# Two 256-column parts of neighbouring head groups computed as one unit of attention scores

## The chip, the core and the metric

The kernel runs on one core of a Trainium2 chip. The metric is the device time of one execution in microseconds (us). The kernel before was timed in three runs: 3645.09, 3648.94 and 3651.80 us, so its median is 3648.94 us. One further execution was profiled; the profile calls the engines PE (TensorE, the matrix engine), DVE (VectorE), ACT (ScalarE), POOL (GpSimd) and SP (SyncE, which issues the DMAs here).

## What is computed

The reference is one transformer block whose norms and residuals are modulated by a condition. Cut to what matters (D = 512, 16 heads of 32 columns, x of shape 8 x 1024 x 512, all in fp32):

```python
def _attention(x, Wqkv, Wproj, bproj):
    ...
    scores = jnp.einsum('bhqd,bhkd->bhqk', q, k) * scale
    causal = jnp.tril(jnp.ones((t, t), bool))
    scores = jnp.where(causal, scores, -jnp.inf)
    attn = jax.nn.softmax(scores, axis=-1)
    ...
    return out @ Wproj + bproj
mod = jax.nn.silu(condition) @ Wada + bada
sh_a, sc_a, gt_a, sh_m, sc_m, gt_m = jnp.split(mod, 6, axis=1)
xm = _layernorm(x, g1, be1) * (1.0 + sc_a[:, None, :]) + sh_a[:, None, :]
x = x + gt_a[:, None, :] * _attention(xm, Wqkv, Wproj, bproj)
xm = _layernorm(x, g2, be2) * (1.0 + sc_m[:, None, :]) + sh_m[:, None, :]
h = jax.nn.gelu(xm @ W1 + b1, approximate=False)
x = x + gt_m[:, None, :] * (h @ W2 + b2)
```

## The kernel before

**Tiling.** The work is cut into 16 blocks of 512 tokens (8 sequences, two halves each). The 16 heads form 4 groups of 4 heads. A head has 32 columns, so the four heads of a group lie on the 128 partitions side by side, and every matmul of the kernel is issued as four small ones that use a quarter of the array each.

**Two kinds of work on PE.** The linear layers (q, k, v, the projection and the two MLP layers, most of them in a scheme with seven products for eight) all go through the helper at L201: tiles of 128 rows and 32 columns of the array, "128*32" in the profile. The scores go through tiles of 32 rows and 128 columns, "32*128" in the profile. Transposes (L641) use the whole array. A run of instructions that all use one of these three shapes is called a stretch below.

**Attention of one group of heads of one block.** It is computed twice. First come the *scores*, which serve only to find the maximum of each row: for each query tile of 128 rows, `scores_at_once` (L1372) writes scores of the four heads into one PSUM tile with the tag `st` (four banks; there is only one such tile), DVE adds the causal mask at the diagonal (L1384) and takes the maxima into the tile `mx` (L1392). Then `split_maxima` (L1406 to L1414) cuts the maxima of a group into three bf16 parts, on DVE or on POOL, whichever the planner believes to be done sooner; PE turns them into rows (L1430) and ACT copies these to SBUF (L1436). Second come the *weights*, transposed: `weights_T` computes the same products with keys as rows (L1456) and subtracts the maxima by a bf16 matmul (L1467), again in the one tile `st`; ACT takes the exponential into a tile `pT` (L1479), POOL clears the part above the diagonal (L1484) and adds the tiles up (L1611), and PE multiplies by v (L1507). `finish` divides by the sums (L1525 to L1557).

**Units.** What is written into `st` at once is a unit. The causal triangle of 512 queries by 512 keys of a group makes three units of scores: query tile 3 with 512 keys; tiles 2 and 0 together with 384 and 128 keys; and tile 1 with 256 keys alone, the half-filled unit. `TRIANGLE` lists them. A block that is the second half of its sequence has four full units more for each group. With 64 groups in all (16 blocks by 4) the profile shows 64 units of 256 columns. The code addresses a part of a unit as (query tile, half of the keys, first column, width).

**What sets the order.** The program is straight-line code. A planner runs when the program is built: it keeps an estimated clock for each engine (`now`), estimated times at which data are written and free (`written`, `left`), and places pieces of linear work (`work`, `step_aside`) between the attention's instructions so that PE has something to do while DVE, ACT or POOL work on `st`. How many units of scores follow a unit of weights is set by `attend`, by the number of units. Engines execute their instructions in the order of the program. If linear work runs out, `scores_by_heads` (L1343) spreads a unit over the three other PSUM banks instead of `st`. For the planner, NEVER marks data that nobody has promised yet; `project_out` of the last block sets it for ("att", last block, tile), and `finish` of the last group replaces it by a time.

Of the kernel before, what the change touches and what calls it, by code (L numbers as in the profile page):

```python
# [9 lines left out]
F32 = mybir.dt.float32  # L10
BF16 = mybir.dt.bfloat16
AF = mybir.ActivationFunctionType
ALU = mybir.AluOpType
AX = mybir.AxisListType
# [8 lines left out]
def kernel(  # L23
# [33 lines left out]
    nc = tc.nc  # L57
    B, T, D = x.shape
    HD = W1.shape[1]
    P = 128  # L60
    hd = D // H
    scale = float(hd) ** -0.5
    TB = 512
    NTT = TB // P
# [3 lines left out]
    HPG = P // hd  # L68
# [13 lines left out]
    small = ctx.enter_context(tc.tile_pool(name="small", bufs=2))  # L82
# [8 lines left out]
    NB = len(blocks)  # L91
# [3 lines left out]
    written, left = {}, {}  # L95
    shape = [None]
    pool_spans = []
    NEVER = float("inf")
# [66 lines left out]
    banks = [ps_l.tile([P, TB], F32, tag=f"l{i}", name=f"bank_{i}") for i in range(3)]  # L165
# [72 lines left out]
    for w in range(1, NB):  # L238
        n = w - 1
# [10 lines left out]
        else:  # L250
# [5 lines left out]
            at = [("at", w + 2)] if w + 2 < NB else []  # L256
# [8 lines left out]
    n = NB - 1  # L265
# [621 lines left out]
    def project_out(n):  # L887
        at = take(NC)
        yield [("attended", n)], []
        attT = qTs[n]  # L890
        tiles = [residual[n][:, t, :] for t in range(NTT)]
        for t, xt in enumerate(tiles):
            xt_job = lambda t=t, xt=xt: add_to(xt, gate_rows["gba"], [("row", "gba")], [("xr", n, t)])
            pool_jobs.append((xt_job, [("xr", n, t)]))
        last = n == NB - 1
        if last:
            for t in range(NTT):
                written["att", n, t] = NEVER
        begun = []

        def begin(t):

            bank = yield from accumulate(
                [(attT[:, c, ts(t, P)], piece(at[c])) for c in range(NC - 1)], [("att", n)], False
            )
            begun.append(bank)

        for t, xt in enumerate(tiles):
            if last:
                while len(begun) <= max(t, 1):  # L910
                    yield from begin(len(begun))
                bank = begun[t]
                yield [("att", n, t)], []
                matmul(
                    banks[bank], attT[:, NC - 1, ts(t, P)], piece(at[NC - 1]), False, True,
                    [("att", n, t)], bank,
                )
            else:
                bank = yield from accumulate(
                    [(attT[:, c, ts(t, P)], piece(at[c])) for c in range(NC)], [("att", n)]  # L920
                )
            y = tmp.tile([P, D], F32, tag="y", name=f"y_{n}_{t}", bufs=2)
            ky = y_key("proj", True)
            combine_out(y, bank, banks[bank], gate_rows["ga"], [("row", "ga")], [ky], ALU.mult)
            if last:
                run_pool_jobs(True)
                nc.vector.tensor_tensor(xt, xt, y, ALU.add)  # L927
                note("DVE", 700, [ky, ("xr", n, t)], [("xr", n, t)], port=True)
                following = normalize_tile(xt, f"m{n}", t, ("xr", n, t))
                if t > 0:  # L930
                    pending()
                pending = following
            else:
                add_to(xt, y, [ky], [("xr", n, t)])
        if last:
            pending()
        release(*at)
        run_pool_jobs(True)
        if not last:
            normalize(tiles, f"m{n}", [("xr", n, t) for t in range(NTT)])  # L940
# [336 lines left out]

    def score_units(n, g):

        h = blocks[n][1]  # L1280
        whole = [[(qt, kh, 0, TB)] for kh in range(h) for qt in range(NTT)]
        for tri in TRIANGLE:
            parts, at = [], 0
            for i in tri:
                w = TB - i * P
                parts.append((NTT - 1 - i, h, at, w))
                at += w
            whole.append(parts)
        return [(n, g, parts) for parts in whole]

# [22 lines left out]
    def keys_of(n, kh):  # L1313
        return kTs[n - blocks[n][1] + kh]

    def scores(n, g, parts):

        h = blocks[n][1]
        if (n, g) not in maxima:
            maxima[n, g] = small.tile([P, 2, NTT, HPG], F32, tag="mx", name=f"mx_{n}_{g}")  # L1320
        mx = maxima[n, g]
        reads = [("qT", n), ("kT", n - h + parts[0][1])]
        if (
            linear_wait() > 3000
            and not any(live)
            and wait_of((reads, ["st"])) > wait_of((reads, [BANK])) + 1000
        ):
            scores_by_heads(n, g, parts, mx, reads)
        else:
            scores_at_once(n, g, parts, mx, reads)  # L1330
        if units[unit_at[0] + 1 :] == [] or units[unit_at[0] + 1][:2] != (n, g):
            split_maxima(n, g, h)

    def scores_by_heads(n, g, parts, mx, reads):

        h = blocks[n][1]
        for some in (range(HPG - 1), range(HPG - 1, HPG)):
            step_aside(reads, [BANK])
            of = {j: lin_bank() for j in some}
            for qt, kh, c0, w in parts:  # L1340
                for j, bank in of.items():
                    r = slice(j * hd, (j + 1) * hd)
                    nc.tensor.matmul(  # L1343
                        banks[bank][:, c0 : c0 + w],
                        qTs[n][r, g, ts(qt, P)],
                        keys_of(n, kh)[r, g, :w],
                        start=True,
                        stop=True,
                        skip_group_check=True,
                    )  # L1350
                note_pe(2 * COLUMN * w, "rows", reads, [("l", bank) for bank in of.values()])
            for j, bank in of.items():
                if parts[0][1] == h:
                    first, span = parts[0][3] - P, len(parts) * P
                    diagonal = banks[bank][:, first : first + span]
                    nc.vector.tensor_tensor(diagonal, diagonal, mask[:, :span], ALU.add)
                    note("DVE", 120 + 1.04 * span, [("l", bank)])
                for qt, kh, c0, w in parts:
                    nc.vector.tensor_reduce(
                        mx[:, kh, qt, j : j + 1], banks[bank][:, c0 : c0 + w], axis=AX.X, op=ALU.max  # L1360
                    )
                    note("DVE", 170 + w, [("l", bank)], [("mx", n, g)])
                live[bank] = False

    def scores_at_once(n, g, parts, mx, reads):
        h = blocks[n][1]
        step_aside(reads, ["st"])
        sc = ps_st.tile([P, HPG, TB], F32, tag="st", name=f"sc_{n}_{g}_{parts[0][0]}_{parts[0][1]}")
        for qt, kh, c0, w in parts:
            for j in range(HPG):  # L1370
                r = slice(j * hd, (j + 1) * hd)
                nc.tensor.matmul(  # L1372
                    sc[:, j, c0 : c0 + w],
                    qTs[n][r, g, ts(qt, P)],
                    keys_of(n, kh)[r, g, :w],
                    start=True,
                    stop=True,
                    skip_group_check=True,
                )
            note_pe(2 * COLUMN * w, "rows", reads, ["st"])  # L1380
        if parts[0][1] == h:
            first, span = parts[0][3] - P, len(parts) * P
            diagonal = sc[:, :, first : first + span]
            nc.vector.tensor_tensor(  # L1384
                diagonal,
                diagonal,
                mask[:, :span].unsqueeze(1).to_broadcast([P, HPG, span]),
                ALU.add,
            )
            note("DVE", 165 + 4.16 * span, ["st"])  # L1390
        for qt, kh, c0, w in parts:
            nc.vector.tensor_reduce(  # L1392
                mx[:, kh, qt, :], sc[:, :, c0 : c0 + w], axis=AX.X, op=ALU.max
            )
            note("DVE", 170 + 4.14 * w, ["st"], [("mx", n, g)])

    def split_maxima(n, g, h):

# [251 lines left out]
        return 600 + 900 * used / TB  # L1650

    def score_need(n, g, parts):
        ns = 300 + sum(100 + 2100 * w / TB for _, _, _, w in parts)
        return ns + (150 + 550 * len(parts) if parts[0][1] == blocks[n][1] else 0)


# [2 lines left out]
    for n in range(NB):  # L1659
        written["attended", n] = NEVER  # L1660
        written["v done", n] = NEVER
        written["m used", n] = NEVER
        if n > 1:
            written["free for v", n] = NEVER
        if n > 2:
            written["free for k", n] = NEVER
    normalize(x_pre.pop(0), "a0", [("x", "a0")] * NTT)
    run_jobs(True)
    open_main([-1], 1.0)
# [65 lines left out]
```

## Time and profile before

| what | value |
|---|---|
| three timed runs, median | 3648.94 us (3645.09 to 3651.80) |
| the profiled execution: its time, its span | 3647.89 us, 3646.2 us |
| PE idle over the span (span less busy time) | 74.6 us |
| DVE, ACT, POOL busy | 2179.1, 1329.2, 2014.6 us |
| instructions on PE (matmuls), DVE, ACT, POOL | 54821, 2501, 1413, 2039 |
| masks added in `st`: 128x512, 128x1024 elements | 128 of 698 ns, 63 of 1230 ns |
| maxima of 256 columns of four heads (128x1024) | 64 of 1225 ns |
| splitting the maxima of a group, four instructions | DVE 42 times, POOL 22 times |
| mean granted clock of PE | 0.995 |

A span is the time from the first to the last instruction of the profiled execution. A group of instructions in the profile is a line of the kernel, an engine, an operation and a form of operands, with how many there were, their busy time in us and the mean of one in ns, and then the idle time of the engine just before them with what ended it. In the trace, an fp32 matmul of the program appears as two, so the four matmuls of one part are "x8". The profile models the end of a matmul; the distance between the starts of two groups is what PE really spent. In a timeline a row has its start in us, its length in us, engine, line, operation, operands and count.

### The profile page before, as it was taken

The numbers are of one execution on the slowest core, as the hardware profiler recorded it, in microseconds if no ns is written. First come the engines' busy times: TensorE is split into PE (matmuls) and PEld (weight loads), VectorE is DVE, ScalarE is ACT, GpSimd is POOL, SyncE is SP. The second block draws the span as 40 slices with busy tenths as digits, with TensorE's granted clock in tenths as the row PEclk, the third lists the DMA queues.
The fourth block names the chain that finished last, engine by engine and source line by source line (L and its number), as shares of the span: only waits on it lengthen the run. The fifth ranks groups of instructions, "written<-read, shape, count | busy, mean of one in ns | idle before, by whom it ended". The sixth has DMA issues, their size and how long they took to land. (4 is left out here: it accounts for less than half of the span.)

```text
span 3646.2 us, 121167 instructions
## 1 busy us (share of the span) xinstructions
PE 3571.6 (98%) x54821; PEld 1770.1 (49%) x54821; DVE 2179.1 (60%) x2501; ACT 1329.2 (36%) x1413; POOL 2014.6 (55%) x2039
## 2 busy tenths in 40 slices
PE   8999999999999999999999999999999999999999
PEld 4434445445554455544545444454544545445445
DVE  6766675564746557465564656746667465664663
ACT  2335234252333523335242352424524244241431
POOL 3656645656455664566636665456654566544560
PEclk9999999999999999999999999999999999999999
DMA  6623333333333343433434334343333433334334
GB/s 220 225 92 104 104 103 109 123 106 119 114 115 112 106 126 111 134 94 104 126 106 143 91 100 123 106 137 103 97 122 110 140 100 103 117 97 143 92 107 138
DMA packets 307894, 430.35 MB, mean 118 GB/s; under 512 B 25900, under 2 KB 176236, under 8 KB 307380
## 3 DMA queue, kind: packets, MB, share of 16 engines
q1 hardware_dynamic: 307264, 422.56, 37.9%
q8 instruction: 432, 7.08, 0.8%
q14 instruction: 82, 0.67, 0.1%
q10 hardware_dynamic: 116, 0.03, 0.0%
HBM read 394.12 MB, written 28.38 MB: 116 GB/s over the span
## 5 line engine op out<-in xcount | busy, mean ns | idle before, releaser
L1611 POOL TENSOR_TENSOR pT<-pT,pT 128x512 f32<-128x512 f32 (+3 forms) x1266 | 1189.2, 973 | 524.9 <-ACT pT L1479 377.1
L1479 ACT ACTIVATE pT<-st 128x2048 f32<-128x2048 f32 (+1 forms) x320 | 546.5, 1708 | 951.3 <-PE st L1467 909.0
L201 PE MATMUL bank<-w,hT 128*32 128x256 f32 x14336 | 808.6, 380 | 2.8 <-DVE hT L1006 2.1
L1392 DVE TENSOR_REDUCE mx<-sc 128x4 f32<-128x1024 f32 (+3 forms) x381 | 664.4, 1757 | 192.4 <-PE sc L1372 185.8
L201 PEld LDWEIGHTS bank<-w,hT 128*32 128x32 f32 x14336 | 452.1, 110 | 354.0 <-issue 58.0
L201 PE MATMUL bank<-xm_m,w 128*32 128x256 f32 x8192 | 506.6, 380 | 0.6 <-ACT rec L1531 0.5
L1484 POOL TENSOR_SCALAR_AFFINE_SELECT pT<-pT 128x512 f32<-128x512 f32 x256 | 175.3, 696 | 576.9 <-ACT pT L1479 576.9
L201 PE MATMUL bank<-t_m,w 128*32 128x256 f32 x6144 | 383.2, 380 | 0.9 <-ACT hT L188 0.9
L201 PEld LDWEIGHTS bank<-xm_m,w 128*32 128x32 f32 x8192 | 253.3, 110 | 252.0 <-issue 98.0
L1456 PE MATMUL st<-qT,kT 32*128 32x512 f32 (+3 forms) x3072 | 339.6, 526 | 21.0 <-DVE mx L1392 20.0
L1372 PE MATMUL sc<-kT,qT 32*128 32x256 f32 (+3 forms) x3048 | 340.6, 527 | 2.9 <-DVE mx L1392 1.9
L1384 DVE TENSOR_TENSOR sc<-sc,mask 128x1024 f32<-128x1024 f32 (+1 forms) x191 | 166.7, 873 | 248.5 <-PE sc L1372 225.5
L1507 PE MATMUL po<-pT,v 128*32 128x512 f32 (+3 forms) x3072 | 312.7, 493 | 2.2 <-POOL pT L1484 1.2
L201 PEld LDWEIGHTS bank<-t_m,w 128*32 128x32 f32 x6144 | 191.9, 110 | 175.7 <-issue 54.2
L201 PE MATMUL bank<-xm_a,w 128*32 128x256 f32 x3968 | 243.5, 381 | 0.0
L201 PE MATMUL bank<-w,qT 128*32 128x512 f32 x2048 | 241.1, 597 | 0.4 <-DVE qT L1547 0.2
L1540 DVE RECIPROCAL rec<-rec 128x128 f32<-128x128 f32 x256 | 224.6, 919 | 8.5 <-ACT rec L1531 8.5
L1456 PEld LDWEIGHTS st<-qT,kT 32*128 32x128 f32 x3072 | 128.9, 184 | 182.7 <-issue 57.5
L1372 PEld LDWEIGHTS sc<-kT,qT 32*128 32x128 f32 x3048 | 126.8, 184 | 161.0 <-ACT pT L1479 77.4
L193 DVE TENSOR_TENSOR hT<-bank,u_u 128x512 f32<-128x512 f32 x192 | 130.2, 686 | 120.9 <-PE bank L201 116.7
L201 PE MATMUL bank<-t_a,w 128*32 128x256 f32 x2944 | 187.2, 382 | 0.0
L1479 ACT ACT_TABLE_LOAD x89 | 114.2, 1283 | 189.3 <-PE st L1467 188.6
(205 smaller groups left out, 3589.5 us busy)
## 6 DMA issues: line engine op xcount, KB each, us to landing
w<-in_L_cond_W_dram SPq DMA_DIRECT2D x384, 256.0 KB, 2.9
w<-kept_up_S SPq DMA_DIRECT2D x256, 256.0 KB, 2.6
w<-kept_down_S SPq DMA_DIRECT2D x256, 256.0 KB, 2.7
w<-kept_qkv_S SPq DMA_DIRECT2D x180, 256.0 KB, 3.0
w<-in_L_cond_Wqkv_dram SPq DMA_DIRECT2D x147, 256.0 KB, 3.3
hat<-in_x_dram SPq DMA_DIRECT2D x64, 256.0 KB, 3.2
w<-in_L_cond_Wproj_dram SPq DMA_DIRECT2D x64, 256.0 KB, 3.8
xr<-in_x_dram SPq DMA_DIRECT2D x64, 256.0 KB, 4.2
```

What stands on the lines that cost most here:

```text
L193: nc.vector.tensor_tensor(out, src, other, op)
L201: nc.tensor.matmul(ps[r, :], lhsT[:, r], rhs, start=start, stop=stop, skip_group_check=True)
L1372: nc.tensor.matmul(sc[:, j, c0 : c0 + w], qTs[n][r, g, ts(qt, P)], keys_of(n, kh)[r, g, :w], start=True, stop=True, skip_group_check=True,)
L1384: nc.vector.tensor_tensor(diagonal, diagonal, mask[:, :span].unsqueeze(1).to_broadcast([P, HPG, span]), ALU.add,)
L1392: nc.vector.tensor_reduce(mx[:, kh, qt, :], sc[:, :, c0 : c0 + w], axis=AX.X, op=ALU.max)
L1456: nc.tensor.matmul(st[:, j, c0 : c0 + w], kT[r, g, ts(k % NTT, P)], qT[r, g, TB - w :], start=(c0 == 0), stop=False, skip_group_check=True,)
L1479: nc.scalar.activation(pT[:, :, :used], st[:, :, :used], AF.Exp, scale=scale)
L1484: nc.gpsimd.affine_select(diagonal, diagonal, pattern=[[0, HPG], [1, P]], compare_op=ALU.is_ge, fill=0.0, base=0, channel_multiplier=-1,)
L1507: nc.tensor.matmul(po[r, TB - w :], v[:, k % NTT, g * P + j * hd : g * P + (j + 1) * hd], pT[:, j, c0 : c0 + w], start=(k == 0), stop=last ...
L1540: nc.vector.reciprocal(some, some)
L1611: nc.gpsimd.tensor_tensor(into, into, pT[:, j, c0 : c0 + w], ALU.add)
```

## The change

The unit of tile 1 alone is dropped for every odd group. For every even group it gets a second part: the same tile 1 with the 256 keys of the next group (odd), so the unit fills all 512 columns of `st`. A part therefore carries its group as a fifth entry, `gg`, and operands and maxima are taken from that group. The mask is added for both halves by one instruction, on a view with a gap (`diagonals`); the maxima are taken by one instruction for each part, as before. The maxima tile of an odd group is thus made while the even group is still open. Because the number of units of a group has changed, the pacing of units in `attend` and the planner's places for all linear work change with it. The mark NEVER for the last block's attention is set at the beginning of the program instead of at the start of `project_out`.

```diff
         for tri in TRIANGLE:
             parts, at = [], 0
             for i in tri:
                 w = TB - i * P
-                parts.append((NTT - 1 - i, h, at, w))
+                parts.append((NTT - 1 - i, h, at, w, g))
                 at += w
+            if tri == [2]:
+                if g % 2:
+                    continue
+                parts.append((*parts[0][:2], at, w, g + 1))
             whole.append(parts)
...
+    def diagonals(parts, sc):
+
+        if parts[-1][4] == parts[0][4]:
+            first, span = parts[0][3] - P, len(parts) * P
+            return span, sc[:, :, first : first + span]
+        return 2 * P, sc.rearrange("p j (a c) -> p j a c", c=2 * P)[:, :, :, P:]
...
-        for qt, kh, c0, w in parts:
+        for qt, kh, c0, w, gg in parts:
             for j in range(HPG):
                 r = slice(j * hd, (j + 1) * hd)
                 nc.tensor.matmul(
                     sc[:, j, c0 : c0 + w],
-                    qTs[n][r, g, ts(qt, P)],
-                    keys_of(n, kh)[r, g, :w],
+                    qTs[n][r, gg, ts(qt, P)],
+                    keys_of(n, kh)[r, gg, :w],
...
-            first, span = parts[0][3] - P, len(parts) * P
-            diagonal = sc[:, :, first : first + span]
-            nc.vector.tensor_tensor(
-                diagonal,
-                diagonal,
-                mask[:, :span].unsqueeze(1).to_broadcast([P, HPG, span]),
-                ALU.add,
+            span, place = diagonals(parts, sc)
+            shape_of = mask[:, :span].unsqueeze(1)
+            if len(place.shape) == 4:
+                shape_of = shape_of.rearrange("p o (a c) -> p o a c", c=P)
+            nc.vector.tensor_tensor(place, place, shape_of.to_broadcast(place.shape), ALU.add)
+            note("DVE", 165 + 4.16 * span, ["st"])
+        for qt, kh, c0, w, gg in parts:
+            nc.vector.tensor_reduce(
+                maxima[n, gg][:, kh, qt, :], sc[:, :, c0 : c0 + w], axis=AX.X, op=ALU.max
             )
...
-        if last:
-            for t in range(NTT):
-                written["att", n, t] = NEVER
...
+    for t in range(NTT):
+        written["att", NB - 1, t] = NEVER
```

`scores_by_heads` is changed in the same way.

More of the change, by code (lines that the diff above doesn't have):

```diff
@@ L1280, in score_units @@
         h = blocks[n][1]
-        whole = [[(qt, kh, 0, TB)] for kh in range(h) for qt in range(NTT)]
+        whole = [[(qt, kh, 0, TB, g)] for kh in range(h) for qt in range(NTT)]
         for tri in TRIANGLE:
@@ L1314, in keys_of @@
         return kTs[n - blocks[n][1] + kh]
+    def diagonals(parts, sc):
[3 more added lines that the diff above has]
+        return 2 * P, sc.rearrange("p j (a c) -> p j a c", c=2 * P)[:, :, :, P:]
     def scores(n, g, parts):
         h = blocks[n][1]
-        if (n, g) not in maxima:
-            maxima[n, g] = small.tile([P, 2, NTT, HPG], F32, tag="mx", name=f"mx_{n}_{g}")
-        mx = maxima[n, g]
+        for gg in {part[4]: None for part in parts}:
+            if (n, gg) not in maxima:
+                maxima[n, gg] = small.tile([P, 2, NTT, HPG], F32, tag="mx", name=f"mx_{n}_{gg}")
         reads = [("qT", n), ("kT", n - h + parts[0][1])]
@@ L1327, in scores, with scores_by_heads @@
         ):
-            scores_by_heads(n, g, parts, mx, reads)
+            scores_by_heads(n, g, parts, reads)
         else:
-            scores_at_once(n, g, parts, mx, reads)
+            scores_at_once(n, g, parts, reads)
         if units[unit_at[0] + 1 :] == [] or units[unit_at[0] + 1][:2] != (n, g):
             split_maxima(n, g, h)
-    def scores_by_heads(n, g, parts, mx, reads):
+    def scores_by_heads(n, g, parts, reads):
         h = blocks[n][1]
@@ L1353, in scores_by_heads, with scores_at_once @@
                 if parts[0][1] == h:
-                    first, span = parts[0][3] - P, len(parts) * P
-                    diagonal = banks[bank][:, first : first + span]
-                    nc.vector.tensor_tensor(diagonal, diagonal, mask[:, :span], ALU.add)
+                    span, place = diagonals(parts, banks[bank].unsqueeze(1))
+                    place = place[:, 0]
+                    shape_of = mask[:, :span]
+                    if len(place.shape) == 3:
+                        shape_of = shape_of.rearrange("p (a c) -> p a c", c=P)
+                    nc.vector.tensor_tensor(place, place, shape_of, ALU.add)
                     note("DVE", 120 + 1.04 * span, [("l", bank)])
-                for qt, kh, c0, w in parts:
+                for qt, kh, c0, w, gg in parts:
                     nc.vector.tensor_reduce(
-                        mx[:, kh, qt, j : j + 1], banks[bank][:, c0 : c0 + w], axis=AX.X, op=ALU.max
+                        maxima[n, gg][:, kh, qt, j : j + 1], banks[bank][:, c0 : c0 + w], axis=AX.X, op=ALU.max
                     )
-                    note("DVE", 170 + w, [("l", bank)], [("mx", n, g)])
+                    note("DVE", 170 + w, [("l", bank)], [("mx", n, gg)])
                 live[bank] = False
-    def scores_at_once(n, g, parts, mx, reads):
+    def scores_at_once(n, g, parts, reads):
         h = blocks[n][1]
@@ L1368, in scores_at_once @@
         sc = ps_st.tile([P, HPG, TB], F32, tag="st", name=f"sc_{n}_{g}_{parts[0][0]}_{parts[0][1]}")
-        for qt, kh, c0, w in parts:
+        for qt, kh, c0, w, gg in parts:
             for j in range(HPG):
@@ L1373, in scores_at_once @@
                     sc[:, j, c0 : c0 + w],
-                    qTs[n][r, g, ts(qt, P)],
-                    keys_of(n, kh)[r, g, :w],
+                    qTs[n][r, gg, ts(qt, P)],
+                    keys_of(n, kh)[r, gg, :w],
                     start=True,
@@ L1381, in scores_at_once @@
         if parts[0][1] == h:
-            first, span = parts[0][3] - P, len(parts) * P
-            diagonal = sc[:, :, first : first + span]
-            nc.vector.tensor_tensor(
-                diagonal,
-                diagonal,
-                mask[:, :span].unsqueeze(1).to_broadcast([P, HPG, span]),
-                ALU.add,
-            )
[L1390 to L1395, printed above, removed]
+            span, place = diagonals(parts, sc)
[4 more added lines that the diff above has]
+            note("DVE", 165 + 4.16 * span, ["st"])
+        for qt, kh, c0, w, gg in parts:
+            nc.vector.tensor_reduce(
+                maxima[n, gg][:, kh, qt, :], sc[:, :, c0 : c0 + w], axis=AX.X, op=ALU.max
+            )
+            note("DVE", 170 + 4.14 * w, ["st"], [("mx", n, gg)])
     def split_maxima(n, g, h):
@@ L1652, in score_need @@
     def score_need(n, g, parts):
-        ns = 300 + sum(100 + 2100 * w / TB for _, _, _, w in parts)
+        ns = 300 + sum(100 + 2100 * w / TB for _, _, _, w, _ in parts)
         return ns + (150 + 550 * len(parts) if parts[0][1] == blocks[n][1] else 0)
```

## The prediction

> **What bounds the kernel now.** I read the busy times first, then what PE waits for, then the timeline of PE around the units that the change touches.
>
> ```profile
> span 3646.2 us, 121167 instructions
> ...
> PE 3571.6 (98%) x54821; PEld 1770.1 (49%) x54821; DVE 2179.1 (60%) x2501; ACT 1329.2 (36%) x1413; POOL 2014.6 (55%) x2039
> ```
>
> PE is busy in all but 74.6 us. No other engine is above 60%, so this is a kernel of PE, and anything on another engine counts only where PE waits for it. The chain of waits agrees but reaches back only to 3531 us. The view of PE's own waits shows how little there is to win by waiting less:
>
> ```profile
> PE st L1456 <- DVE mx L1392: 20.0, 35, 1.9
> PE bank L409 <- ACT cond_act L403: 6.5, 1, 6.5
> ...
> PE bank L1343 <- DVE mx L1359: 4.3, 2, 3.7
> ...
> PE bank L1430 <- DVE mcols L1414: 2.1, 1, 2.1
> ```
>
> (us in total, times, longest.) The largest entry is weights waiting for the one tile `st` until DVE has taken the maxima: 20 us in 35 places.
>
> **Inside "busy" there is time without work.** This is the timeline of PE around one half-filled unit:
>
> ```profile
> 769.49 1.91 PE L201 MATMUL bank<-xm_m,w 128*32 128x256 f32 x32
> 771.21 1.05 PE L201 MATMUL bank<-t_m,w 128*32 128x256 f32 x16
> 772.19 0.71 PE L1372 MATMUL sc<-kT,qT 32*128 32x256 f32 x8
> 772.83 1.07 PE L201 MATMUL bank<-t_m,w 128*32 128x256 f32 x16
> 773.72 1.05 PE L201 MATMUL bank<-xm_m,w 128*32 128x256 f32 x16
> ```
>
> Look at starts, not lengths. 32 matmuls in one shape take 771.21 - 769.49 = 1.72 us, so 16 take 0.86 and 8 take 0.43. The 16 ahead of the scores take 0.98 (0.12 too long), the 8 of the scores 0.64 (0.21 too long), the 16 behind them 0.89 (0.03 too long). Entering and leaving the other shape costs 0.36 us, nearly as much as the unit's own 0.43. The same three excesses return at every lone unit that I looked at, and with 512 columns too (1.07 us instead of 0.86), so the price belongs to the stretch and not to its length.
>
> **Part 1: fewer stretches on PE.** No matmul goes; 32 units do. In the program orders of both kernels I counted changes of shape: 636 stretches of 32*128 before, 605 after (31 fewer; one merged unit goes by heads). 31 x 0.36 = 11.2 us. The planner's new order also bunches the transposes: 93 stretches of the whole array before, 77 after. In the timelines one transpose between L201 groups takes 0.26 us and two 0.37, so 0.11 each and 0.15 fixed; the eight L201 matmuls before take 0.57 instead of 0.43. That is 0.30 a stretch, and 16 x 0.30 = 4.8 us. **Sum: 16.0 us of PE time, all on the bound.**
>
> [...]
>
> **Part 2: the mask and the maxima on DVE.** From the groups by form:
>
> ```profile
> L1384 DVE TENSOR_TENSOR sc<-sc,mask 128x512 f32<-128x512 f32 x128 | 89.3, 698 | 172.3 <-PE sc L1372 158.0 <-issue 13.8 <-ACT hat L580 0.3
> ...
> L1392 DVE TENSOR_REDUCE mx<-sc 128x4 f32<-128x1024 f32 x64 | 78.4, 1225 | 2.2
> L1384 DVE TENSOR_TENSOR sc<-sc,mask 128x1024 f32<-128x1024 f32 x63 | 77.5, 1230 | 76.3 <-PE sc L1372 67.5 <-ACT rec L1531 4.4 <-ACT top L1534 1.9
> ```
>
> 64 masks of 698 ns become 31 of 1230: 6.6 us less on DVE, which is not the bound. (The view with a gap is not in the trace; I price it as the mask without gap, between 0.70 for half of it and 1.40 for two.) What matters is how long `st` is held. The unit of 384+128 columns has the same mask and as many columns, and shows it:
>
> ```profile
> 933.66 1.15 PE L1372 MATMUL sc<-kT,qT 32*128 32x384 f32 x16
> ...
> 934.95 1.23 DVE L1384 TENSOR_TENSOR sc<-sc,mask 128x1024 f32<-128x1024 f32 x1 [0.89 <-PE sc L1372]
> ...
> 936.22 2.36 DVE L1392 TENSOR_REDUCE mx<-sc 128x4 f32<-128x1536 f32 x2
> ...
> 938.72 1.15 PE L1456 MATMUL st<-qT,kT 32*128 32x384 f32 x16 [0.88 <-DVE mx L1392]
> ```
>
> From 933.66 to 938.72 are 5.06 us, 1.08 of them the unit's own; PE needs 3.98 us of other work before the next use of `st`, or it waits, here 0.88. [...] By the row it costs about nothing: in the new order, 29 of the 31 merged units have 4.2 us or more of other PE work behind them, against 3.98. The other two have 3.7 and 2.7, a loss of 1.6 us. The 384+128 units that have 4.2 us today share what is left of the 20.0 us when the larger entries are taken off, about 0.03 us each: 0.9 us for the 29.
>
> **Part 3: waits that move with the new order.** Before, seven places wait 0.73 us because DVE makes two subtractions of 1.8 us (L1006) ahead of the mask of a lone unit; in the new order the merged unit's maxima stand ahead of them: -5.1. Seven places with 3.3 us behind a 384+128 unit (0.87 each) become six with 2.8 (1.2 each): +0.9. Six places have 2.06 us between two units of weights, where the next one needs 0.49 until the exponential starts, 1.88 for it and 0.1 for its signal, less the 0.33 of L1467 itself, 2.14: +0.6.
>
> **Part 4: the split of the maxima goes to POOL.** Of 64 groups, DVE did 42 and POOL 22; in the new order 10 and 54. A split is 621+823+532+429 ns on DVE and 255+229+253+268 ns on POOL, so DVE loses 77 us and POOL gets 32, neither on the bound. But an even group's maxima are now complete one reduction (1.22 us) later. From the merged unit's end: 0.2 + 1.23 + 2.45 + 0.18 + 1.0, about 5.2 us with signals. Ten groups have 5.5 us until L1430, 18 more up to 6.1. POOL adds in steps of 1.31 us (L1611) and is 55% busy: I take 0.2 us for each of the ten, +2.0. Ends: nothing, or one addition in the way of all 28, about 1 us each.
>
> **Part 5: the rest.** NEVER issues nothing, and from the last sums (L1525) on the PE order is the same: 0. Its wait for POOL, 1.57 us, has 0.4 us less work ahead. SP issues the same 1622 instructions; from block 2 on no transfer is moved. In the first two blocks the transfers that prepare sums of MLP weights come later, by one stage of four loads and four stores.
>
> **Part 6: the shortage of linear work in block 1.** There the projection waits for the last attention of block 0, whose division stands in DVE's queue behind scores:
>
> ```profile
> 180.00:190.00 10.00, 6.49 (x22) 2.80 (x26) 9.79 (x19) 0.00 (x0) 0.64 (x3) 0.50 0.98 318
> 190.00:200.00 10.00, 8.16 (x46) 2.41 (x50) 8.88 (x9) 2.00 (x2) 5.86 (x6) 0.50 0.24 94
> ```
>
> (Busy us of PE, PEld, DVE, ACT, POOL; granted clock; DMA.) DVE is full and PE at half clock. From the maxima of the full unit at 173.53 us to the last reciprocal's end at 196.77, DVE takes 23.2 us. In the new order the same stretch of its queue, priced by the same rows, sums to 25.4: the merged unit goes by heads there, and brings the next group's part along. POOL has seven preparing subtractions ahead of the quotient in both. +2.2, and by the clock up to 8 us either way.
>
> Waits: -5.1 + 0.9 + 0.6 + 1.6 + 0.9 + 2.0 + 2.2 = +3.1. Sum: -16.0 + 3.1 = -12.9. The profiled execution, 3647.9 us, becomes 3635.0; the median lies 1.05 above it, so **3636 us**.
>
> **The rivals.**
> - *Gain given back, 3648 us.* The new waits of parts 2 to 4 reach their upper half (0.5 us at 28 groups is 14 us, 2 of them already counted). For: `st` is single, and the same waits recur in each period of two blocks. Against: waits cost 20 us in all now.
> - *Slower, 3662 us: the split behind POOL's additions.* L1430 stands in PE's order, so everything behind it waits. At 28 groups, 0.5 us each eats the gain, and beyond (12.9 + 7.3) / 28 = 0.7 us it decides; one addition of 1.31 us each, less 0.3 of slack and the 2.0 counted, gives 3662. For: a unit's exponential releases four additions at once, 5.2 us of POOL in order. Against: today's 22 splits on POOL found it idle, waiting for DVE (125.7 us before L1411), and PE waits for none.
> - *The shortage in block 1 passes at full clock, 3628 us.* For: PE gets more small matmuls between the scores there in the new order. Against: DVE is full and its queue longer.
> [...]
>
> **Chances and range.** Forecast 0.59, its own range 3628 to 3642 (the clock, and 5 us for waits); given back 0.13; slower 0.16; block 1 at full clock 0.07; small price 0.05. A measurement here tells 0.2% (7.3 us) from no change: faster 0.59 + 0.07 = 0.66, same 0.13 + 0.05 = 0.18, slower 0.16. The range 3619 to 3653 leaves out the slower case and little else.
>
> **What would show it.** PE's busy time should fall by some 16 us and its idle time stay near 75; a merged unit should take 1.07 us from start to start; L1456 should wait near 20 us in all, L1430 for POOL under 5. The forecast is wrong if PE's idle time grows by more than 8 us, above all at L1430, or if busy time falls by 5 only.

## The result, and the profile after

| | before | after |
|---|---|---|
| time, median of 20 runs each on the same chip, us | 3648.47 (3644.62 to 3651.8) | 3642.8 (3639.35 to 3645.55) |
| ratio, 95% interval | | 0.9985 [0.9978, 0.9992] |
| span of the profiled execution, us | 3646.2 | 3640.9 |

The change brings 5.7 us, 0.15%: a real gain by its interval, but less than half of the 12.9 us forecast, just outside of the forecast's own range (3628 to 3642), and within the 0.2% that the prediction called no change.

The head of the page and the engines' busy times, after:

```profile
span 3640.9 us, 121132 instructions
...
PE 3556.7 (98%) x54821; PEld 1769.6 (49%) x54821; DVE 2123.4 (58%) x2351; ACT 1330.3 (37%) x1421; POOL 2042.9 (56%) x2147
```

PE's busy time fell by 3571.6 - 3556.7 = 14.9 us, close to the 16.0 of the forecast (the part on why comes back to this). But its idle time, span less busy, rose from 74.6 to 84.2 us: +9.6 where +3.1 was forecast. That is over the 8 us which the prediction named as the sign that it is wrong. The view of what PE waits for, after (us in total, times, longest):

```profile
PE po L1517 <- POOL pT L1494: 14.3, 10, 2.0
PE st L1466 <- DVE mx L1402: 11.7, 18, 1.4
PE bank L641 <- ACT xm_m L651: 7.1, 6, 1.2
PE bank L1353 <- DVE mx L1372: 6.8, 3, 4.8
...
PE bank L1440 <- POOL mcols L1424: 3.8, 3, 1.6
...
PE bank L201 <- ACT xm_m L651: 3.0, 7, 0.4
```

The lines have moved by 10 or so: L1466 is L1456 of before, L1440 is L1430, L1517 is L1507, L1494 is L1484, L1385, L1399 and L1402 are L1372, L1384 and L1392. The wait of `st` for DVE fell from 20.0 to 11.7 us, more than forecast. In its place stands an entry that before had 1.2 us:

```profile
PE po L1507 <- POOL pT L1484: 1.2, 2, 1.1
```

The sums of the attention (`po`) now wait 14.3 us for POOL, which clears the keys of the future (`pT`, L1494). The prediction has no term for it.

**Where along the run.** The borders are the starts of the sums of weights (L1525 before, L1535 after) of the same stages. In each of the six periods PE has the same 6784 matmuls to do in both kernels, so the change of stretches, priced as in part 1, can be set beside them in the last column. Across the other borders linear work has moved, and the column says how much. Us:

| part of the run | before | after | by the price of stretches, or work moved |
|---|---|---|---|
| start to the end of block 0 | 170.9 | 165.7 | 21 matmuls fewer |
| to block 2, group 2 | 349.3 | 345.4 | 45 matmuls more |
| six periods of two blocks each | 446.1, 445.1, 445.9, 448.3, 445.1, 445.1 | 445.1, 445.3, 450.3, 447.8, 446.7, 446.7 | -1.6 in the first, -1.9 to -2.0 in the others |
| to the last sums | 324.0 | 319.7 | 24 matmuls fewer |
| from there to the end | 126.4 | 128.2 | none moved |

The gain lies in the first 520 us (-9.1) and ahead of the last sums (-4.3); behind them 1.8 us are lost. In the six periods between, where 11.2 us should have been won, 6.3 were lost.

**The wait that eats it.** This is the timeline of after (start, duration, engine, line, in square brackets the idle time before) around the first long one of the ten waits:

```profile
1244.39 2.35 DVE L1402 TENSOR_REDUCE mx<-sc 128x4 f32<-128x1024 f32 x2
1246.63 0.26 POOL L1421 CAST mcols<-mx 128x16 bf16<-128x16 f32 x1
...
1247.60 0.27 POOL L1424 TENSOR_TENSOR mcols<-rest,mcols 128x16 bf16<-128x16 f32 x1
1247.78 5.19 POOL L161 TENSOR_TENSOR xr<-xr,row_gbm 128x512 f32<-128x512 f32 x3
1247.86 1.75 DVE L158 TENSOR_TENSOR xr<-xr,row_gbm 128x512 f32<-128x512 f32 x1
...
1248.42 1.88 ACT L1489 ACTIVATE pT<-st 128x2048 f32<-128x2048 f32 x1 [6.85 <-PE st L1477]
...
1249.53 4.53 DVE L1003 TENSOR_TENSOR hT<-hT 128x1024 f32<-128x1024 f32 x2
...
1252.93 1.62 POOL L1494 TENSOR_SCALAR_AFFINE_SELECT pT<-pT 128x512 f32<-128x512 f32 x1
...
1254.60 1.06 PE L1517 MATMUL po<-pT,v 128*32 128x512 f32 x8 [1.95 <-POOL pT L1494]
```

The exponential ends at 1250.30 and the clearing could begin. But POOL is in the middle of three additions of the gated bias of the MLP (`row_gbm`). The clearing starts behind them, at 1252.93, and PE waits for it from 1252.65 to 1254.60. The four additions of this stage are free to run on either engine, as `either` finds the shorter queue in the plan. The clearing itself is slow here too: it takes 1.62 us while DVE makes its subtractions (L1003), and 0.64 in before, where DVE stood idle beside it. With 0.64 the wait of 1.95 us would be about 1 us shorter (an estimate from these two rows). Before, at the same stage, three additions were on DVE and one on POOL, and the clearing came as soon as the exponential was done:

```profile
1257.24 5.08 DVE L158 TENSOR_TENSOR xr<-xr,row_gbm 128x512 f32<-128x512 f32 x3
1261.73 1.72 POOL L161 TENSOR_TENSOR xr<-xr,row_gbm 128x512 f32<-128x512 f32 x1
...
1271.12 0.64 POOL L1484 TENSOR_SCALAR_AFFINE_SELECT pT<-pT 128x512 f32<-128x512 f32 x1 [2.28 <-ACT pT L1479]
```

Over the run, 43 of the 64 such additions are on POOL after, 38 before. At five places, one for every two blocks, the wait is 1.95 to 1.97 us, 9.8 us in all.

**What follows on the wait.** Behind three of these five waits the granted clock falls. The view by windows of after at one of them (us; busy us and count of PE, PEld, DVE, ACT, POOL; granted clock; DMA share; GB/s):

```profile
1700.00:1704.00 4.00, 2.04 (x36) 0.78 (x32) 2.69 (x2) 3.97 (x7) 3.92 (x3) 1.00 0.20 66
1704.00:1708.00 4.00, 4.00 (x48) 2.04 (x44) 0.00 (x0) 3.96 (x4) 4.00 (x4) 0.57 0.00 0
```

PE is idle for 1.96 us in the first window; in the second it is busy all the time at a mean clock of 0.57, and does 48 matmuls, where the window from 1256 to 1260 in after has 80 at a clock of 1.00. The clock is 0.50 from 1704.14 to 1707.55 and 1.00 in the 3.41 us on either side. So 3.41 us are run at half clock, 1.7 us lost, nearly as much as the wait itself. With the three places that makes 5.1 us, hidden in "busy".

### The profile page after: what moved, and what is told of

The parts are those of the page before. It is cut to its first block, busy times and chain, and to the rows that moved or that the text cites. A ratio compares the mean times of both kernels' runs of the same rounds, so it can differ in the third digit from the quotient of the medians.

```text
span 3640.9 us, 121132 instructions
## 1 busy us (share of the span) xinstructions
PE 3556.7 (98%) x54821; PEld 1769.6 (49%) x54821; DVE 2123.4 (58%) x2351; ACT 1330.3 (37%) x1421; POOL 2042.9 (56%) x2147
## 5 line engine op out<-in xcount | busy, mean ns | idle before, releaser
L1621 POOL TENSOR_TENSOR pT<-pT,pT 128x512 f32<-128x512 f32 (+3 forms) x1266 | 1208.1, 988 | 541.0 <-ACT pT L1489 402.6
L1402 DVE TENSOR_REDUCE mx<-sc 128x4 f32<-128x2048 f32 (+3 forms) x381 | 660.9, 1755 | 170.7 <-PE sc L1385 165.1
L1494 POOL TENSOR_SCALAR_AFFINE_SELECT pT<-pT 128x512 f32<-128x512 f32 x256 | 176.9, 703 | 568.0 <-ACT pT L1489 567.7
L1466 PE MATMUL st<-qT,kT 32*128 32x512 f32 (+3 forms) x3072 | 339.1, 526 | 12.7 <-DVE mx L1402 11.7
L1385 PE MATMUL sc<-kT,qT 32*128 32x512 f32 (+3 forms) x3048 | 329.4, 522 | 4.3 <-ACT pT L1489 2.4
L1399 DVE TENSOR_TENSOR sc<-sc,mask 128x1024 f32<-128x1024 f32 (+1 forms) x159 | 161.5, 1016 | 288.6 <-PE sc L1385 227.9
L1517 PE MATMUL po<-pT,v 128*32 128x512 f32 (+3 forms) x3072 | 312.0, 492 | 14.7 <-POOL pT L1494 14.3
L1466 PEld LDWEIGHTS st<-qT,kT 32*128 32x128 f32 x3072 | 127.6, 183 | 186.8 <-issue 85.2
L1385 PEld LDWEIGHTS sc<-kT,qT 32*128 32x128 f32 x3048 | 129.3, 184 | 158.1 <-ACT pT L1489 87.5
L193 DVE TENSOR_TENSOR hT<-bank,u_u 128x512 f32<-128x512 f32 x192 | 128.8, 684 | 111.6 <-PE bank L201 110.8
L201 PEld LDWEIGHTS bank<-xm_a,w 128*32 128x32 f32 x3968 | 122.9, 110 | 107.5 <-issue 36.9
```

Source lines behind the costliest of these rows:

```text
L193: nc.vector.tensor_tensor(out, src, other, op)
L201: nc.tensor.matmul(ps[r, :], lhsT[:, r], rhs, start=start, stop=stop, skip_group_check=True)
L1385: nc.tensor.matmul(sc[:, j, c0 : c0 + w], qTs[n][r, gg, ts(qt, P)], keys_of(n, kh)[r, gg, :w], start=True, stop=True, skip_group_check=True,)
L1399: nc.vector.tensor_tensor(place, place, shape_of.to_broadcast(place.shape), ALU.add)
L1402: nc.vector.tensor_reduce(maxima[n, gg][:, kh, qt, :], sc[:, :, c0 : c0 + w], axis=AX.X, op=ALU.max)
L1466: nc.tensor.matmul(st[:, j, c0 : c0 + w], kT[r, g, ts(k % NTT, P)], qT[r, g, TB - w :], start=(c0 == 0), stop=False, skip_group_check=True,)
```

## Experiments

The theory: the merge is worth about what its stretches say, and the plan's three additions on POOL take it away. The rivals: the price of a stretch was too high; or moving the split of the maxima to POOL (part 4) is to blame. Each kernel has five or eleven timed runs. The runs of the kernel before beside them gave 3648.77 us for the first four kernels and 3649.35 us for the last three. After was not timed again beside them; differences to it are differences to the 3642.8 us above.

### The additions left out

Within `either`, POOL's branch issues nothing where the four additions of the gated MLP bias call it; the plan and the order on PE stay as they are. So the 43 additions that the plan put on POOL are missing in the residual.

```diff
-            nc.gpsimd.tensor_tensor(out, a, b, op)
+            if not as_planned[0]:
+                nc.gpsimd.tensor_tensor(out, a, b, op)
...
+            as_planned[0] = True
             for i in range(NTT):
                 add_to(residual[n][:, i, :], gate_rows["gbm"], ...)
+            as_planned[0] = False
```

> The changed kernel, program of PE unchanged; the additions of the gated bias of the second layer (xr + row_gbm) that the new order gives to POOL are left out, so the residual lacks that bias there. Theory A (the gain is given back because these additions, three in a row of 1.73 us each, stand on POOL ahead of the clearing of pT, for which PE waits at L1517: 14.3 us in 10 places): that wait falls below 3 us, the half-clock windows behind it go, and the time falls by 13 to 17 us to 3626 to 3630 us, ratio to before about 0.994. Theory B (the gain is given back because the merged unit holds the one tile st longer): nothing changes for st, so 3643 us, ratio 0.9985.

Measured: 3624.68 us (3622.83 to 3625.08), ratio to before 0.9934 [0.9921, 0.9948], 18 us under after. The wait, in this kernel's view of PE's waits:

```profile
PE po L1521 <- POOL pT L1498: 3.5, 4, 1.5
```

14.3 us have become 3.5; idle time is 71.3 us and, outside of the first 520 us, 3.4 us run at half clock instead of 21.9. So these 43 instructions, 128x512 each and none of them waited for, cost 18 us. They could do it by holding POOL up or by delaying what needs the residual; the next two runs tell that.

### The same additions on DVE

```diff
-            nc.gpsimd.tensor_tensor(out, a, b, op)
+            place = nc.vector if as_planned[0] else nc.gpsimd
+            place.tensor_tensor(out, a, b, op)
```

> The changed kernel, program of PE unchanged; the additions that the new order gives to POOL are issued on DVE at the same place. Theory A: the wait at L1517 for POOL falls below 4 us, but DVE is then 3 to 5 us late with L1003 and the maxima behind it, so PE waits there, as it did before: 3632 to 3643 us, ratio 0.9955 to 0.9985. Theory B: 3643 us.

Measured: 3628.06 us (3627.34 to 3629.56), ratio 0.9945 [0.9932, 0.9957], 14.7 us under after with all the work of after and its PE order. It was better than the 3632 to 3643 us expected.

```profile
PE po L1521 <- POOL pT L1498: 3.5, 4, 1.4
...
PE st L1470 <- DVE mx L1406: 12.7, 17, 1.4
```

The wait for POOL falls as if the additions were gone, and the wait of `st` for DVE grows by 1.0 us only (11.7 to 12.7). It is POOL's queue, not the residual, that PE waited for. DVE had been expected to be late, and was not. This is the stage shown above:

```profile
1248.12 1.28 DVE L163 TENSOR_TENSOR xr<-xr,row_gbm 128x512 f32<-128x512 f32 x2
...
1250.53 2.79 DVE L1005 TENSOR_TENSOR hT<-hT 128x1024 f32<-128x1024 f32 x2
...
1250.64 1.60 POOL L1498 TENSOR_SCALAR_AFFINE_SELECT pT<-pT 128x512 f32<-128x512 f32 x1 [2.50 <-ACT pT L1493]
```

With POOL idle beside it, DVE adds in 0.64 to 0.69 us, where its one addition in after took 1.75 beside POOL's three. So its four additions and two subtractions end 4.64 us after the start of the exponential, against 5.64 for one addition and the same subtractions in after. The clearing is as slow as in after (1.60 us), but it begins when the exponential ends, and PE doesn't wait for it here. Its late start, not its length alone, made the wait.

### The same additions on POOL, but later

In `down` they go into the list of POOL's small jobs, which the planner hands out one at a time, and what is left of them is forced at the start of the second part of `down`:

```diff
             for i in range(NTT):
-                add_to(residual[n][:, i, :], gate_rows["gbm"], [("row", "gbm")], [("xr", n, i)])
+                pool_jobs.append((
+                    lambda i=i: add_to(
+                        residual[n][:, i, :], gate_rows["gbm"], [("row", "gbm")], [("xr", n, i)]
+                    ),
+                    [("xr", n, i)],
+                ))
...
+            run_pool_jobs(True)
```

> The changed kernel with the same four additions of a block not in a row at the start of the second layer, but one at a time when POOL is free, at the latest before the second quarter of that layer. All work is done. Theory A: as without the additions, less a few us for what they now delay: 3628 to 3636 us, ratio 0.995 to 0.997, with less than 5 us of wait at L1517 for POOL. Theory B: 3643 us, ratio 0.9985.

Measured: 3620.54 us (3619.86 to 3623.3), ratio 0.9925 [0.9913, 0.9938]. This beats both kernels: 28 us under before, 22 under after. Its engines and the top of its view of waits:

```profile
PE 3550.3 (98%) x54821; PEld 1772.3 (49%) x54821; DVE 2107.3 (58%) x2350; ACT 1330.5 (37%) x1422; POOL 2041.7 (56%) x2147
```

```profile
PE st L1472 <- DVE mx L1408: 10.1, 15, 1.1
PE bank L641 <- ACT xm_m L651: 7.1, 6, 1.2
```

POOL has as many instructions as after (2147) and the same busy time (2041.7 against 2042.9), and 43 of the additions are still on it. Only their place differs. At the stage shown above the timeline of this kernel now has

```profile
1248.09 0.64 POOL L1500 TENSOR_SCALAR_AFFINE_SELECT pT<-pT 128x512 f32<-128x512 f32 x1 [2.50 <-ACT pT L1495]
```

that is, POOL idle for 2.50 us until the exponential ends, and the clearing done in 0.64 us instead of 1.62, with DVE's subtractions ended before it. (The plan shifts with the edit, so some linear work on PE stands elsewhere than in after; the two runs before this one have after's order.)

### The same edit without the merge

The kernel before, with that edit and the early mark NEVER, which alone leaves the program before as it is, instruction for instruction.

> The kernel before with the same edit (additions one at a time when POOL is free) and the early NEVER mark, without the merged unit. Before, three of the additions went to DVE, ahead of L1006 and the mask of a lone unit: 0.36 + 0.73 us of wait in seven places. Theory A: the edit alone is worth at most these 8 us here, 3640 to 3645 us (ratio 0.998 to 0.999), and the merge on top of it is worth the 10 us or more that the forecast gave it. Theory B: the edit is worth about the same with and without the merge, and the merge on top of it stays below 7 us.

Measured: 3644.63 us (3640.76 to 3646.26), ratio 0.9987 [0.9978, 0.9996]. On the kernel before, the edit is worth 4 us; with it in both, the merge brings 3644.63 - 3620.54 = **24.1 us**. The same parts of the run as in the first table:

| | edit alone | edit and merge | difference | by the price of stretches, or work moved |
|---|---|---|---|---|
| start to the end of block 0 | 171.0 | 165.6 | -5.4 | 21 matmuls fewer |
| to block 2, group 2 | 350.4 | 344.5 | -5.9 | 45 matmuls more |
| six periods | 445.9, 444.9, 445.9, 447.8, 444.9, 444.9 | 443.8, 443.1, 445.7, 445.3, 442.9, 442.9 | -2.1, -1.8, -0.2, -2.5, -2.0, -2.1 | -1.6, then -1.9 to -2.0 |
| to the last sums | 320.0 | 315.3 | -4.6 | 64 matmuls fewer |
| from there to the end | 127.2 | 128.6 | +1.4 | 40 matmuls more |

In five of six periods the merge now gives its -1.8 to -2.5, as the price of part 1 has it. No period of either kernel has half clock, and PE's busy time falls in all six, by 1.8 to 2.1 us, 12.1 in all; in the third its idle time grows by 1.9. The 24.1 us are more than the price: over the whole run busy time falls by 20.6 us and idle time by 4.6, and 14.6 us less are run at half clock (38.5 and 23.9), worth up to 7.3 us. That last part lies in the first 520 us and near the end of the run, and its share of the gain was not tried by an edit.

### One more change of shape in every merged unit

Four matmuls of eight columns in the other shape are put between the two halves of each of the 31 merged units; in a control, the same four stand ahead of the unit, where the shape changes anyway. Plan and order are those of after.

```diff
+        def small_columns(at):
+            for j in range(HPG):
+                r = slice(j * hd, (j + 1) * hd)
+                nc.tensor.matmul(
+                    sc[r, 0, at : at + 8], minus_ones[:, r], ident_b[:, :8], ...
+                )
         for qt, kh, c0, w, gg in parts:
+            if gg != g:             # first kernel
+                small_columns(c0)
...
+        if parts[-1][4] != g:       # control, ahead of the loop
+            small_columns(0)
```

> The changed kernel with four tiny matmuls of the shape 128*32 (8 columns, overwritten at once by the unit) between the two parts of each merged unit: the same plan, 31 stretches more on PE. [...]

> The changed kernel with the same four tiny matmuls ahead of each merged unit, where PE mostly is in the shape 128*32 already: no stretch more. [...]

Measured: 3645.93 us (3643.61 to 3647.54) with the extra change of shape, 3644.93 us (3643.22 to 3648.05) for the control. The timeline of PE at one merged unit, first with the extra change, then in the control:

```profile
904.60 1.90 PE L201 MATMUL bank<-w,qT 128*32 128x512 f32 x16
906.43 0.71 PE L1395 MATMUL sc<-kT,qT 32*128 32x256 f32 x8
907.08 0.19 PE L1385 MATMUL sc<-ident_b,minus_ones 128*32 128x8 bf16 x4
907.20 0.71 PE L1395 MATMUL sc<-kT,qT 32*128 32x256 f32 x8
907.84 1.50 PE L201 MATMUL bank<-xm_a,w 128*32 128x256 f32 x24
```

```profile
902.32 1.90 PE L201 MATMUL bank<-w,qT 128*32 128x512 f32 x16
904.04 0.19 PE L1385 MATMUL sc<-ident_b,minus_ones 128*32 128x8 bf16 x4
904.16 1.15 PE L1395 MATMUL sc<-kT,qT 32*128 32x256 f32 x16
905.23 1.07 PE L201 MATMUL bank<-xm_a,w 128*32 128x256 f32 x16
```

From the 16 ahead to the linear work behind are 3.24 us in the one and 2.91 in the other. After has 2.91 too (901.13 to 904.04), so the small matmuls vanish in the change of shape, and one more stretch costs 0.33 us, the small matmuls in it included. The price of part 1 (0.36) is thereby measured by adding one, at the place where it is paid.

Yet the total does not show it: the two medians differ by 1.0 us, within their spread, not by 31 x 0.33 = 10.2, nor by the 31 x 0.36 = 11 of part 1's price. The profiles show where it went. First with the extra change, then the control:

```profile
PE po L1527 <- POOL pT L1504: 12.2, 10, 1.6
```

```profile
PE po L1527 <- POOL pT L1504: 14.4, 10, 2.0
```

PE arrives later where another engine sets the time: the five long waits are 1.95 to 1.97 us in the control and 1.62 to 1.64 with the extra change, shorter by one stretch, and the wait of `st` for DVE falls too, from 11.9 to 9.6 us. In each of the first three periods, with four merged units, busy time grows by 1.2 us, idle time falls by 0.6, and the period is 0.5 or 0.6 us longer. And behind the shorter waits the clock does not fall: in the last three periods the control has 3.4 us each at half clock, or 5.1 us of work lost in all, and the kernel with the extra change none, so there it is the shorter one by 1.1 or 1.2 us. So where another engine's queue sets a point in each period, a part of the time that PE saves ahead of it is waited for behind, as in the merge itself.

### The splits back on DVE

```diff
-        engine = nc.gpsimd if on_pool else nc.vector
+        engine = nc.vector
```

The plan still takes them to be on POOL.

> The changed kernel, order of PE unchanged; all splits of the maxima are issued on DVE where the plan has 54 of them on POOL (POOL some 50 us less, DVE 100 us more). Forecast's rival (the splits behind POOL's additions hold PE up): the waits for POOL at L1440 (3.8 us) and L1517 (14.3 us) fall and the time with them, to about 3630 us. Theory A (the waits at L1517 come from the additions of the gated bias alone): L1517 keeps 12 us or more, DVE gets later, 3643 to 3655 us.

Measured: 3664.35 us (3664.19 to 3666.7), ratio 1.0045 [1.0032, 1.0057], 21.6 us more than after. The view of PE's waits in this kernel:

```profile
PE bank L1440 <- DVE hT L193: 20.6, 7, 3.4
...
PE st L1466 <- DVE mcols L1421: 6.7, 8, 0.9
...
PE po L1517 <- POOL pT L1494: 2.9, 2, 1.5
```

The wait for the clearing falls from 14.3 to 2.9 us, since the additions start sooner without a split ahead of them and are out of the way. But PE now waits for DVE instead: at the stage shown above the split takes 4.4 us there (1250.89 to 1255.31) against 1.24 on POOL (1246.63 to 1247.87). L1440 needs the split as weights and, going by its releaser in the view, also a bank that DVE empties at L193, behind the split in its queue. It stands in PE's order and stops everything behind it. Five such waits are of 3.40 us. The split is this slow where POOL makes its three additions beside it (1250.89 to 1254.60); the medians of its four instructions over the run, 0.20, 0.19, 0.20 and 0.23 us on DVE, are no longer than POOL's. At this place the split is better on POOL. How much of the wait at L1517 in after is the split's, and how much the additions' behind it, this run does not separate.

## Why the prediction was right or wrong

**Part 1, fewer stretches: right in kind, and in size where it can be seen alone.** With the edit in both kernels, PE's busy time falls by 12.1 us in the six periods, which have the same matmuls and no half clock; the price says 11.2. A stretch measured by adding one costs 0.33 us. The 14.9 us of the whole run, against 16.0, agree less well than they seem to: 7.3 us less of after are run at half clock (39.4 and 32.1), and that alone can be up to 3.7 us of the fall. No run shows the small price to which the prediction gives a chance of 0.05, nor the fall of busy time by 5 us only that goes with it: the added stretch cost 0.33 us, and busy time fell by 12.1 us in the six periods.

**Part 2, mask and maxima: right.** After, the merged unit takes 1.08 us from start to start, the mask on the view with a gap 1.23 us, and `st` is held for 5.10 us (forecast 1.07, 1.23 and 5.06):

```profile
1241.84 1.15 PE L1385 MATMUL sc<-kT,qT 32*128 32x256 f32 x16
...
1242.92 1.93 PE L201 MATMUL bank<-xm_m,w 128*32 128x256 f32 x32
...
1243.12 1.23 DVE L1399 TENSOR_TENSOR sc<-sc,mask 128x1024 f32<-128x1024 f32 x1 [0.46 <-PE sc L1385]
...
1246.94 1.14 PE L1466 MATMUL st<-qT,kT 32*128 32x512 f32 x8
```

**Part 3, the waits that move: here it failed.** The term is -5.1 + 0.9 + 0.6. It follows the waits on `st` through the new order, and for those it was too careful: with the 1.6 and 0.9 of part 2 it makes -1.1 us, and that entry fell by 8.3. But it counts DVE's queue alone. What the planner moves with the order, the additions that either engine may take, was not followed: "the wait at L1507 for POOL" is nowhere in the sum, since it stood at 1.2 us. It became 14.3, and half clock behind it cost another 5. A smaller new entry is the wait at L641 for `xm_m`, 7.1 us at six places; as other waits of L641 fell, all of them together rose from 12.0 to 14.6 us.

**Part 4, the split on POOL: right in what it denied.** PE waits 3.8 us at L1440 (forecast: under 5), so the rival that ends on the slower side did not come in this form. Its mechanism, a thing needed soon that stands behind POOL's additions in order, was the right one, though it had the additions of L1611 in mind and not those of the bias. It struck one instruction later, at the clearing. The prediction had asked whether additions stand ahead of the split, and not what stands ahead of the clearing when a split and three additions go first.

**Part 5: right for NEVER**, as the programs are the same with and without it. The part behind the last sums, put at 0, grew by 1.8 us (126.4 to 128.2); it has 11.6 us at half clock against 8.7, worth up to 1.5 of them.

**Part 6, the shortage in block 1: wrong in sign.** +2.2 was taken, with 8 us either way; that part of the run became 3.9 us shorter (5.9 in the pair with the edit) although 45 more matmuls fall into it. The DVE queue from the maxima of the full unit to the end of the last reciprocal took 20.0 us after (172.43 to 192.45), against 23.2 before and 25.4 forecast: the next full unit's maxima, 2.29 us, which stood ahead of the last reciprocal (193.62), now come behind it (201.10). Half clock in the first 520 us was 23.9 us before, 10.2 after, and 17 to 24 in the six other kernels with the merge, so how much of the gain is the clock differs from kernel to kernel. This was read and not tried by an edit.

**Small slips in the sums** change nothing: 64 masks of 698 ns less 31 of 1230 are 6.5 us, not 6.6, and six times 0.08 us are 0.5, not 0.6.

**The total.** The rival of the gain given back (3648) is the nearest in kind: waits rose by 9.6 us, though not at the places that it named. The time lies between it and the forecast because block 1, the wait of `st` and the part ahead of the last sums gave more than was counted. That these made up for a part of a loss that no term named, and kept the time 7 us from the forecast, is luck.

## What to carry to other kernels

When a scheduler places work anew, compare the queue of every engine ahead of each instruction that PE waits for, also of those that wait for nothing today; work which "may go on either engine" is the first to wander. Three additions issued in one go were 5.2 us of POOL's queue ahead of something urgent; handed out one at a time, the same additions showed no cost. Look also at what DVE and POOL do side by side: here an addition on DVE took 0.64 to 0.69 us alone and 1.75 beside POOL's additions, and the clearing on POOL 0.64 alone and 1.62 beside DVE's subtractions. And look at the granted clock behind a wait of PE: here three of the five waits of 1.95 to 1.97 us in after were followed by 3.41 us at half clock, which made them cost nearly twice their length.

## What of the hardware was not expected

**DVE and POOL side by side.** An addition of 128x512 took 0.64 to 0.69 us on DVE with POOL idle (the kernel with the same additions on DVE), and 1.75 beside POOL's additions (after). The clearing on POOL took 0.64 us with DVE idle and 1.60 to 1.62 beside DVE's subtractions. Not every company goes with it: beside DVE's L193, which reads one operand from a bank, the clearing keeps 0.63 us (median of 76 in after). No experiment was made on the cause.

**The clock.** In after, a wait of PE of 1.95 to 1.97 us was followed by 3.41 us at half clock at three of five places, with the same neighbours; waits of 3.40 us, in the kernel with the splits on DVE, at all five:

```profile
1252.00:1256.00 4.00, 0.60 (x13) 0.17 (x9) 3.90 (x6) 3.25 (x3) 3.92 (x5) 0.94 0.20 61
1256.00:1260.00 4.00, 4.00 (x52) 1.68 (x52) 4.00 (x4) 2.94 (x5) 4.00 (x3) 0.63 0.00 0
```

The control of the extra change of shape has the five waits of 1.95 us too, and again half clock behind three. Where the longest wait in these periods is at most 1.54 us (the additions left out, on DVE, or later) or 1.64 (the extra change of shape), no half clock was seen there.

The traces also show at which. Apart from the last one, which the end of the execution cuts, the times at half clock in after are 3.41 or 6.83 us long, those in before 23.89, 6.83 and 6.83. Within one execution their starts lie whole numbers of 3.413 us apart: in after the three behind the waits are 1704.14, 2598.43 and 3045.58, and 894.29 and 447.15 us are 262 and 131 such steps. Lay steps of that length over the ten waits of 1.95 us in after and the control: six lie whole within one step, and the next step after each is at half clock; four are cut by a border between two steps, and behind none of them the clock falls. The wait shown first (1252.65 to 1254.60) is cut at 1253.58 and leaves PE 0.93 us idle in one step and 1.02 in the next:

```profile
1250.16:1253.58 3.42, 2.49 (x44) 1.13 (x36) 3.42 (x2) 3.39 (x6) 3.42 (x3) 1.00 0.30 77
1253.58:1256.99 3.41, 2.39 (x36) 1.20 (x40) 0.47 (x1) 3.38 (x4) 3.33 (x3) 1.00 0.02 5
```

So in these ten waits, of two executions, the fall of the clock goes with their place against the steps. This was read and not tried by an experiment; whether the place decides stays open.
